# Score tiles in runs of two, three and three, and one shared set of PSUM banks, in a fused attention block

## The chip, the core and the metric

The kernel runs on one core of one Trainium2 chip. The metric is the device time of one execution in microseconds (us). Smaller is better.

## What is computed

Four sequences of 1024 tokens with 1024 features go through conditioned attention with 16 heads, a residual, and a causal convolution with four taps whose taps are the condition vectors:

```python
scale, shift = split(emb @ W_emb + b_emb)
xn = rms_norm(x, g_norm) * (1 + scale) + shift
q, k, v = heads(xn @ W_qkv)                  # 16 heads of 64
q, k = rms_norm(q, g_q), rms_norm(k, g_k)
attn = softmax(q @ k.T * 64 ** -0.5)
o = attn @ v
x = x + (o + o @ W_out)
x = x + causal_conv(x, taps=cond, bias=conv_b)   # 4 taps, per feature
```

Everything is float32.

## The kernel before

**Work.** The projection to q, k and v is done in 16 doubles (four for each sequence, two pairs of heads in each). A double is cut into seven products P1 to P7 of half-size blocks, which are combined by additions, each for four token tiles. That makes 28 pieces, and a piece (`Double.piece`, L638) is one PSUM tile `pqkv` of 128 x 384: eight TensorE instructions, then the additions that empty it (L657 to L669, on ScalarE for P1, on VectorE for the others). Transposes of q and k (`qkt`, L500), transposed inputs (`xtp`, L310), the output projection (`po`, L927 and L1004, begun by the transposed residual of L991) and the transposes ahead of a store (`otp`, L1051) use one PSUM bank each as well. All these tiles come from one pool of three banks, `ps_m`.

**Attention.** It goes in 64 units. A unit p is one pair of heads and one half (512) of the queries of a sequence. The text calls its eight key tiles S0 to S7 where scores are meant, and V0 to V7 where values are.

- `scores` (L683): for each key tile two matmuls, one for each head of the pair, side by side in the halves of the array (64 rows each), into one tile of two PSUM banks (`ps_s`, two such tiles), copied to `sp` in SBUF by ScalarE in one instruction of 128 x 1024 (L696). A running maximum over the key tiles follows on VectorE (L705).
- `softmax` (L732) only plans: the maximum over partitions on GpSimd (L710), its copy into a third use of `ps_s`, called `mbp` (L719), then for each key tile a subtraction on VectorE (L724), an exponential on ScalarE and a running sum on GpSimd (L728, L730).
- `values` (L746): 16 matmuls side by side in the two column halves of the array, into the bank of `ps_a`.
- `finish` (L760): `tot`, the sums over the keys, in a bank of `ps_m`. `spread` (L781) copies them out, `invert` (L791) and `divide` (L799) send the reciprocal through DRAM and multiply.

So PSUM's eight banks are four for `ps_s`, three for `ps_m`, one for `ps_a`.

**Order.** The order of instructions on every compute engine is the order in which the program emits them. The emission is steered by a clock of estimated times: `defer(delay, key, step)` puts a step off, `tick(us)` moves the clock and emits what has come due, `need(key)` emits the named steps at once. A tile of a pool waits until the last reader of the bank's earlier tile is done.

The main loop (L1322 to L1357) emits, for unit p, its scores in four runs of two key tiles, between them the values of unit p-1 (0 to 3, then 4 and 5, then 6 and 7), `finish`, and then, behind the last scores, the fill: the pieces of `between(p)` (L1235), which hold seven projection pieces, transposes, output products and the loads of later ones. `split` (L1273) keeps the last 26 us of the pieces by the clock (22 us for the first 16 units) behind the scores, and what is over is cut into three stretches that go between the runs.

In unit 63 the fill consists of `own`, seven tiles of the output projection of the last sequence. After the loop come the values of unit 63, its `finish` and `divide`, and nine more output tiles. Each output tile is `residual`, two products, two ScalarE instructions that read the bank (`L1019`, `L1033`), and afterwards usually one `otp` of an earlier tile.

Of the kernel before, what the change touches and what calls it, by code (L numbers as in the profile page):

```python
# [15 lines left out]
P = 128  # L16
# [5 lines left out]
def kernel(  # L22
# [53 lines left out]
    small = ctx.enter_context(tc.tile_pool(name="small", bufs=2))  # L76
    ps_s = ctx.enter_context(tc.tile_pool(name="ps_s", bufs=2, space=bass.MemoryType.PSUM))
    ps_m = ctx.enter_context(tc.tile_pool(name="ps_m", bufs=3, space=bass.MemoryType.PSUM))
    dram = ctx.enter_context(tc.tile_pool(name="dram", bufs=1, space=bass.MemoryType.DRAM))
# [62 lines left out]

    turn = [0]

    def evacuate(dst, src):

        turn[0] ^= 1
        if turn[0]:
            nc.scalar.copy(dst, src)
        else:  # L150
            nc.vector.tensor_copy(dst, src)

# [26 lines left out]
    cols_ps = ps_m.tile([P, 512], F32, tag="m", name="cols_ps")  # L179
    nc.tensor.transpose(cols_ps[:, :NR], rows, ident[:NR, :NR])  # L180
# [83 lines left out]
    class Chunk:  # L264
# [31 lines left out]
        def transposes(self, c):  # L296
            b, k, q = self.b, self.k, self.q
            need("xg", self.name)
            if c == 0:
                if len(combining) == 2:  # L300
                    d, *at = combining.pop(0)
                    need(*(("r", d, *at) if d else ("s", *at)))
                combining.append((b, q, k))
                tag, n, bufs = R_HOMES.get((q, k), R_HOME) if b == 0 else R_HOME
                rs = [
                    apool.tile([P, n, QN], F32, tag=tag, name=f"r_{self.name}_{i}", bufs=bufs) for i in range(0, 8, n)
                ]
                self.r = lambda i: rs[i // n][:, i % n, :]
                self.stores = [(rs[i // n][:, : min(n, 7 - i), :], i, min(i + n, 7)) for i in range(0, 7, n)]
            tp = ps_m.tile([P, 2, QN], F32, tag="m", name=f"xtp_{self.name}_{c}")  # L310
# [70 lines left out]
    class Embed:  # L381
# [22 lines left out]
        def run(self):  # L404
            half = self.half
            ps = ps_m.tile([P, 512], F32, tag="m", name=f"mod_ps_{half}")[:, :QN]
            for k in range(NJ):
# [10 lines left out]

            mt = ps_m.tile([P, 512], F32, tag="m", name=f"modT_ps_{half}")[:, :QN]
            mt = mt.rearrange("p (i g b) -> p i g b", i=2, g=4)  # L420
# [27 lines left out]
    class Pair:  # L448
# [51 lines left out]
        def transposes(self, g, s):  # L500

            b, c = self.b, self.c
            need("qk", b, c, g)
            tp = ps_m.tile([P, HN], F32, tag="m", name=f"qkt_{b}_{c}_{g}_{s}")
# [81 lines left out]
    class Double:  # L586
# [39 lines left out]
        def direct(self, c, q):  # L626

            a = self.a[(A11, A12)[c], q] = self.tile_a((A11, A12)[c], q)
            for k in range(KH):
                tp = ps_m.tile([P, 512], F32, tag="m", name=f"xtd_{c}_{q}_{k}")[:, :QN]  # L630
                for i in range(2):
                    nc.tensor.transpose(
                        tp[:, i * P : (i + 1) * P], x0[2 * q + i][c][:, k * P : (k + 1) * P], ident
                    )
                tick(0.22)
                modulate(a[:, k, :], tp, 0, k + c * KH, k % 2 == 1)

        def piece(self, i):  # L638

            name, place, t = self.products[i]  # L640
            px, py = self.pairs
            pm = ps_m.tile([P, 512], F32, tag="m", name=f"pqkv_{self.n}_{name}_{t}")[:, :W3]
            w, a = self.w[name], self.a.get((place, t // 2))
# [33 lines left out]
    class Unit:  # L677
# [5 lines left out]
        def scores(self, kts):  # L683
            pr = self.pr
            for kt in kts:
                ps = ps_s.tile([P, 2, HN], F32, tag="s", name=f"s_{self.name}_{kt}")
                for h in range(2):
                    nc.tensor.matmul(  # L688
                        ps[:, h, :],
                        pr.kT[kt // HT][h * D : (h + 1) * D, kt % HT * P : (kt % HT + 1) * P],  # L690
# [4 lines left out]
                sp = apool.tile([P, 2, HN], F32, tag="sp", name=f"sp_{self.name}_{kt}", bufs=9)  # L695
                nc.scalar.copy(sp, ps)  # L696
                self.sp.append(sp)
# [19 lines left out]
        def broadcast(self):  # L717
            mb = ps_s.tile([P, 2, HN], F32, tag="s", name=f"mbp_{self.name}")
            nc.scalar.copy(mb, self.mb)  # L719
# [177 lines left out]
    class Quad:  # L897
# [29 lines left out]
        def product(self, name):  # L927
# [9 lines left out]
            else:  # L937
                pm = ps_m.tile([P, 512], F32, tag="m", name=f"po_{b}_{j}_{name}")
            for k in range(KH):
# [23 lines left out]
    class Out:  # L963
# [27 lines left out]
        def residual(self, whole=False):  # L991

            self.pm = ps_m.tile([P, 512], F32, tag="m", name=f"po_{self.name}")
            for i in range(HT):
# [56 lines left out]
        def store(self):  # L1051
            b, j, half = self.b, self.j, self.half
            need("y", self.name)
            tp = ps_m.tile([P, 512], F32, tag="m", name=f"otp_{self.name}")
            for i in range(HT):
# [15 lines left out]
    TO_MAX, TO_SPREAD, TO_SHIFT, TO_EXP, STEP = 2.6, 6.5, 7.6, 1.3, 1.8  # L1071
    BEHIND = 26
    SHARES = (0.25, 0.5, 0.25)
    LEADS = ((11, 7), (10, 9))
    LEADS_LAST = ((11, 7), (10, 12))
    DIVIDE = 18.0
    STEP_FIRST = 1.6
    BEHIND_FIRST = 22.0
    LATER = ((0, 0), (4, 0))
# [174 lines left out]

    def cut(pieces, shares):

        ends = list(accumulate(shares))
        total = sum(t for t, _ in pieces)
        stretches, done = [[] for _ in shares], 0.0
        for t, step in pieces:  # L1260
            at = (done + t / 2) / max(total, 1e-9) * ends[-1]
            stretches[next((i for i, e in enumerate(ends) if at < e), len(ends) - 1)].append((t, step))
            done += t
        return stretches
# [8 lines left out]
    def split(pieces, behind):  # L1273

        left, n = behind, len(pieces)
        while n and left > 0:
            n -= 1
            left -= pieces[n][0]
        return cut(pieces[:n], SHARES) + [pieces[n:]]


# [41 lines left out]
    for p in range(B * NB):  # L1323
        unit = Unit(doubles[p // 4].pairs[p // 2 % 2], p % 2)
        stretches = split(between(p), BEHIND if p >= NB else BEHIND_FIRST)
        if p == B * NB - 1:
# [3 lines left out]
            gather(B - 1, 1)  # L1330
            stretches = cut(between(p), SHARES) + [own]
        stretches = iter(stretches)

        def fill():
            run(next(stretches))
# [68 lines left out]
```

## Time and profile before

| | |
|---|---|
| median of 3 runs | 2846.8 us (2844.96 to 2851.01) |
| profiled execution, first to last instruction | 2846.5 us; the page gives no other time of it |
| TensorE (PE) busy | 2764.2 us, 97% |
| VectorE (DVE) busy | 2161.3 us, 76% |
| ScalarE (ACT) busy | 1541.5 us, 54% |
| GpSimd (POOL) busy | 1345.1 us, 47% |
| mean granted TensorE clock | 0.995 |

The profile names an instruction by its engine, its line in the kernel and the tiles it writes and reads. "PE" is a matmul and "PEld" the loading of weights for it. A float32 matmul shows as two TensorE instructions, so a pair of score matmuls for one key tile is four. The chain that ended last goes back from the last instruction to whatever released each step. The list of waits gives, for each group of instructions, the idle time of its engine ahead of it and what ended that. The timeline merges neighbouring instructions of a line and gives their start and the length up to the end of the last one; since matmuls overlap, the time that a run takes is the distance of its start from the start of the next row.

### The profile page before, as it was taken

Reading aid. Unit: us, or ns where it says so; the run is one execution under the profiler, and the core shown is the slowest. Engines: PE = TensorE matmul, PEld = TensorE weight load, DVE = VectorE, ACT = ScalarE, POOL = GpSimd, SP = SyncE. Lnnn points to the kernel's source line nnn. Section 1 sums busy time; section 2 is a strip of 40 time slices with the busy share of each in tenths; the row PEclk is TensorE's granted clock in tenths of the full one; section 3 lists DMA queues with packets and bytes.
Section 4 is the critical chain, followed back from the end, with each engine's and each line's share of the span. In section 5 each row is a group of like instructions: output and inputs, shape, how many; then the busy total and the mean of one; then the engine's idle time right before and its main releaser. Section 6 shows DMA issues by size and latency. Waiting matters only on the chain.

```text
span 2846.5 us, 31973 instructions
## 1 busy us (share of the span) xinstructions
PE 2764.2 (97%) x10581; PEld 1310.7 (46%) x10581; DVE 2161.3 (76%) x2579; ACT 1541.5 (54%) x2221; POOL 1345.1 (47%) x534
## 2 busy tenths in 40 slices
PE   6999999999999999999999999999999999999998
PEld 3544444444444444444444445445444444443344
DVE  4688887888888777777877777787877877687863
ACT  4255656655555556655555556665555545555532
POOL 2056554565654453553555355355445445554520
PEclk9999999999999999999999999999999999999999
DMA  9844555644565566665565556666556444533334
GB/s 318 280 168 145 193 174 184 211 152 169 174 196 159 174 196 205 214 229 164 162 207 186 165 178 212 203 218 198 163 202 211 141 130 159 167 109 96 118 108 118
DMA packets 416844, 509.40 MB, mean 179 GB/s; under 512 B 40816, under 2 KB 326824, under 8 KB 406952
## 3 DMA queue, kind: packets, MB, share of 16 engines
q1 hardware_dynamic: 416680, 507.36, 55.1%
q8 instruction: 85, 1.39, 0.2%
q14 instruction: 79, 0.65, 0.1%
HBM read 411.85 MB, written 95.40 MB: 178 GB/s over the span
## 4 chain that ended last, share of the span: by engine, by line
PE 78%; DVE 11%; DMA 4%; ACT 3%; issue 2%; POOL 2%; SPq 1%; DVEq 0%; ACTq 0%; POOLq 0%
PE pqkv_P L648 29%; PE pav L751 15%; PE s L688 15%; PE po L1009 5%; PE po_P L940 4%; PE po L940 4%; DVE sp L724 3%; DVE mx L705 3%; POOL sum L730 1%; PE qkt L506 1%; PE tot L766 1%; DMA scrR<-few 1%; DVE qk L498 1%; PE po L995 1%; ACT sp L696 1%
## 5 line engine op out<-in xcount | busy, mean ns | idle before, releaser
L648 PE MATMUL pqkv_P<-w_P,a 128*128 128x384 f32 x3456 | 1172.5, 490 | 15.5 <-issue 5.6
L730 POOL TENSOR_TENSOR sum<-sum,sp 128x1024 f32<-128x1024 f32 x384 | 956.8, 2492 | 36.5 <-ACT sp L728 5.7
L648 PEld LDWEIGHTS pqkv_P<-w_P,a 128*128 128x128 f32 x3456 | 639.4, 190 | 478.7 <-issue 69.2
L696 ACT COPY sp<-s 128x1024 f32<-128x1024 f32 x512 | 506.0, 1015 | 507.4 <-PE s L688 459.1
L705 DVE TENSOR_TENSOR mx<-mx,sp 128x1024 f32<-128x1024 f32 x384 | 518.9, 1351 | 170.9 <-ACT sp L696 143.8
L728 ACT ACTIVATE sp<-sp 128x1024 f32<-128x1024 f32 x512 | 531.8, 1055 | 204.6 <-DVE sp L724 201.3
L724 DVE TENSOR_TENSOR sp<-sp,mbp 128x1024 f32<-128x1024 f32 x512 | 604.2, 1210 | 19.3 <-ACT mbp L719 19.3
L710 POOL PARTITION_ALL_REDUCE mb<-mx x64 | 219.2, 3426 | 826.5 <-DVE mx L705 785.0
L688 PE MATMUL s<-qT,kT 64*128 64x512 f32 x2048 | 516.3, 620 | 21.8 <-DVE sp L724 17.0
L751 PE MATMUL pav<-sp,v 128*64 128x512 f32 x2048 | 486.5, 607 | 0.0
L730 POOL TENSOR_TENSOR sum<-sp,sp 128x1024 f32<-128x1024 f32 x64 | 151.5, 2367 | 485.6 <-ACT sp L728 232.9
L688 PEld LDWEIGHTS s<-qT,kT 64*128 64x128 f32 x2048 | 174.9, 186 | 314.8 <-issue 200.0
L751 PEld LDWEIGHTS pav<-sp,v 128*64 128x64 f32 x2048 | 131.2, 137 | 331.9 <-issue 322.2
L1045 DVE SCALAR_TENSOR_TENSOR y<-x,cols,y 128x512 f32<-128x512 f32 x192 | 224.3, 1173 | 47.9 <-ACT y L1033 43.3
L705 DVE TENSOR_TENSOR mx<-sp,sp 128x1024 f32<-128x1024 f32 x64 | 113.2, 1769 | 102.1 <-ACT sp L696 102.0
L667 DVE TENSOR_TENSOR qk<-u,pqkv_P 128x256 f32<-128x256 f32 x256 | 106.2, 415 | 77.9 <-PE pqkv_P L648 76.5
L1009 PE MATMUL po<-ob,wo 128*128 128x512 f32 x352 | 155.3, 593 | 0.0
L940 PE MATMUL po_P<-o_P,wq_P 128*128 128x512 f32 x320 | 143.9, 592 | 0.0
L498 DVE TENSOR_TENSOR qk<-qk,ms 128x1024 f32<-128x1024 f32 x64 | 129.7, 2047 | 0.0
L719 ACT COPY mbp<-mb 128x1024 f32<-128x1024 f32 x64 | 65.2, 1018 | 111.0 <-POOL mb L710 111.0
L940 PE MATMUL po<-o_P,wq_P 128*128 128x512 f32 x240 | 108.0, 592 | 0.0
L485 ACT ACTIVATE sq<-qk 128x512 f32<-128x512 f32 x128 | 76.7, 627 | 53.6 <-DVE qk L667 53.6
(94 smaller groups left out, 1730.7 us busy)
## 6 DMA issues: line engine op xcount, KB each, us to landing
a<-scrA SPq DMA_DIRECT2D x212, 512.0 KB
w_P<-scrB SPq DMA_DIRECT2D x64, 768.0 KB
o_P<-scrS SPq DMA_DIRECT2D x40, 1024.0 KB
w_P<-in_L_cond_W_qkv_dram SPq DMA_DIRECT2D x192, 192.0 KB
o_P<-scrO SPq DMA_DIRECT2D x30, 1024.0 KB
scrA<-r SPq DMA_DIRECT2D x28, 896.0 KB
wq_P<-scrW SPq DMA_DIRECT2D x70, 256.0 KB
xc<-in_x_dram SPq DMA_DIRECT2D x64, 256.0 KB
```

Source lines behind the costliest of these rows:

```text
L648: nc.tensor.matmul(pm, (chunk.r(place) if a is None else a[:, k, :])[:, t % 2 * P : (t % 2 + 1) * P], w[:, k, :], start=(k == 0), stop=(k ...
L688: nc.tensor.matmul(ps[:, h, :], pr.kT[kt // HT][h * D : (h + 1) * D, kt % HT * P : (kt % HT + 1) * P], pr.qT[self.half][h * D : (h + 1) * ...
L696: nc.scalar.copy(sp, ps)
L705: nc.vector.tensor_max(self.mx, self.mx if kt > 1 else self.sp[0], self.sp[kt])
L710: nc.gpsimd.partition_all_reduce(self.mb.rearrange("p h q -> p (h q)"), self.mx.rearrange("p h q -> p (h q)"), P, bass_isa.ReduceOp.max,)
L724: nc.vector.tensor_sub(self.sp[kt], self.sp[kt], self.mb)
L728: nc.scalar.activation(sp, sp, AF.Exp)
L730: nc.gpsimd.tensor_tensor(self.sum, self.sum if kt > 1 else self.sp[0], sp, ALU.add)
L751: nc.tensor.matmul(self.pav[h * D : (h + 1) * D, :], self.pr.v[kt // HT][:, kt % HT, h * D : (h + 1) * D], self.sp[kt][:, h, :], start=(kt ...
L940: nc.tensor.matmul(pm, self.w[name][:, k, :], self.o[name][:, k, :], start=(k == 0 and name not in ("P2", "P3", "P4")), stop=(k == KH - 1),)
L1009: nc.tensor.matmul(self.pm, self.w[kh][:, k % KH, :], oTs[b, k, half], start=False, stop=(k == NJ - 1),)
L1045: nc.vector.scalar_tensor_tensor(self.y, self.x1[:, k : k + HN], cols[:, r : r + 1], self.y, ALU.mult, ALU.add)
```

## The change

- The pools `ps_s` and `ps_m` become one pool in which every bank has a name: `s0` and `s1` (two banks each), `b0`, `b1` and `m` (one each).
- Scores: key tiles 0, 3, 6 use `s1`, key tiles 1, 4, 7 use `s0`, and key tiles 2 and 5 use the two single banks `b0` and `b1`, one for each head, with one copy of 128 x 512 for each instead of one of 128 x 1024.
- `mbp` is always in `s0`.
- All other PSUM tiles come from `bank()`, which goes round a list: all five names up to the first scores, `m` alone during the scores, `m`, `b0`, `b1` in the fill, and `b0`, `b1` from the fill of the last unit to the end.
- The runs are two, three and three key tiles, with values 0 to 3 and 4 to 7 between them, and the whole of `between(p)` comes behind the last scores.
- What is left of the subtractions and exponentials of unit p-1 is emitted ahead of S0, not behind S1. `spread` is emitted with `finish`.

```diff
-    ps_s = ctx.enter_context(tc.tile_pool(name="ps_s", bufs=2, space=bass.MemoryType.PSUM))
-    ps_m = ctx.enter_context(tc.tile_pool(name="ps_m", bufs=3, space=bass.MemoryType.PSUM))
+    psum = ctx.enter_context(tc.tile_pool(name="psum", bufs=1, space=bass.MemoryType.PSUM))
...
+    def double_bank(i, name):
+        return psum.tile([P, 2, 512], F32, tag=f"s{i}", name=name)
+
+    APART = ["m"]
+    FILL = ["m", "b0", "b1"]
+    ALL = FILL + ["s1", "s0"]
+    banks, at_bank = [ALL], [0]
+
+    def use_banks(some):
+        banks[0], at_bank[0] = some, 0
+
+    def bank(name):
+        tag = banks[0][at_bank[0] % len(banks[0])]
+        at_bank[0] += 1
+        if tag[0] == "s":
+            return double_bank(int(tag[1]), name)[:, 0, :]
+        return psum.tile([P, 512], F32, tag=tag, name=name)
...
-            pm = ps_m.tile([P, 512], F32, tag="m", name=f"pqkv_{self.n}_{name}_{t}")[:, :W3]
+            pm = bank(f"pqkv_{self.n}_{name}_{t}")[:, :W3]
...
-                ps = ps_s.tile([P, 2, HN], F32, tag="s", name=f"s_{self.name}_{kt}")
+                name = f"s_{self.name}_{kt}"
+                if kt % 3 == 2:
+                    ps = [psum.tile([P, HN], F32, tag=f"b{h}", name=f"{name}_{h}") for h in range(2)]
+                else:
+                    whole = double_bank(1 - kt % 3, name)
+                    ps = [whole[:, h, :] for h in range(2)]
...
-                nc.scalar.copy(sp, ps)
+                if kt % 3 == 2:
+                    for h in range(2):
+                        nc.scalar.copy(sp[:, h, :], ps[h])
+                else:
+                    nc.scalar.copy(sp, whole)
...
-            mb = ps_s.tile([P, 2, HN], F32, tag="s", name=f"mbp_{self.name}")
+            mb = double_bank(0, f"mbp_{self.name}")
...
-            tot = ps_m.tile([P, HN], F32, tag="m", name=f"tot_{self.name}")
+            tot = bank(f"tot_{self.name}")
...
-            defer(0.2, key, lambda: self.spread(tot))
+            self.spread(tot)
...
-        stretches = split(between(p), BEHIND if p >= NB else BEHIND_FIRST)
+        pieces = between(p)
         if p == B * NB - 1:
...
-            stretches = cut(between(p), SHARES) + [own]
...
+            pieces += own
+
+        use_banks(APART)
+        if last is not None:
+            need("exp", last.name)
         unit.scores((0, 1))
         if last is not None:
-            need("exp", last.name)
             last.values(range(0, HT))
-        fill()
-        unit.scores((2, 3))
-        fill()
+        unit.scores((2, 3, 4))
         if last is not None:
-            last.values(range(4, 6))
-        unit.scores((4, 5))
-        if last is not None:
-            last.values(range(6, NT))
+            last.values(range(HT, NT))
             last.finish()
-        fill()
-        unit.scores((6, 7))
+        unit.scores((5, 6, 7))
+        use_banks(FILL if p < B * NB - 1 else FILL[1:])
         need("mx", unit.name)
         unit.softmax()
...
-        fill()
+        run(pieces)
         last = unit
```

The other tiles of `ps_m` (`xtp`, `qkt`, `po`, `otp` and a few at the start) go over to `bank()` in the same way as `pqkv`.

More of the change, by code (lines that the diff above doesn't have):

```diff
@@ L2 @@
 from contextlib import ExitStack
-from itertools import accumulate, count
+from itertools import count
 import concourse.bass as bass
@@ L141, in need @@
         flush(lambda e: e[2] == key)
[L143 to L151, printed above, removed]
+    def double_bank(i, name):
[12 more added lines that the diff above has]
+        return psum.tile([P, 512], F32, tag=tag, name=name)
     def inverse_root(x, n):
@@ L178 @@
             nc.sync.dma_start(rows[R_GQ + i : R_GQ + i + 1, h * D : (h + 1) * D], g.rearrange("(o d) -> o d", o=1))
-    cols_ps = ps_m.tile([P, 512], F32, tag="m", name="cols_ps")
+    cols_ps = bank("cols_ps")
     nc.tensor.transpose(cols_ps[:, :NR], rows, ident[:NR, :NR])
@@ L309, in transposes @@
                 self.stores = [(rs[i // n][:, : min(n, 7 - i), :], i, min(i + n, 7)) for i in range(0, 7, n)]
-            tp = ps_m.tile([P, 2, QN], F32, tag="m", name=f"xtp_{self.name}_{c}")
+            tp = bank(f"xtp_{self.name}_{c}").rearrange("p (h t) -> p h t", h=2)
             for i in range(4):
@@ L405, in run @@
             half = self.half
-            ps = ps_m.tile([P, 512], F32, tag="m", name=f"mod_ps_{half}")[:, :QN]
+            ps = bank(f"mod_ps_{half}")[:, :QN]
             for k in range(NJ):
@@ L417, in run @@
             nc.scalar.copy(sb, ps)
-            mt = ps_m.tile([P, 512], F32, tag="m", name=f"modT_ps_{half}")[:, :QN]
+            mt = bank(f"modT_ps_{half}")[:, :QN]
             mt = mt.rearrange("p (i g b) -> p i g b", i=2, g=4)
@@ L503, in transposes @@
             need("qk", b, c, g)
-            tp = ps_m.tile([P, HN], F32, tag="m", name=f"qkt_{b}_{c}_{g}_{s}")
+            tp = bank(f"qkt_{b}_{c}_{g}_{s}")
             for i in range(HT):
@@ L629, in direct @@
             for k in range(KH):
-                tp = ps_m.tile([P, 512], F32, tag="m", name=f"xtd_{c}_{q}_{k}")[:, :QN]
+                tp = bank(f"xtd_{c}_{q}_{k}")[:, :QN]
                 for i in range(2):
@@ L685, in scores @@
             for kt in kts:
-                ps = ps_s.tile([P, 2, HN], F32, tag="s", name=f"s_{self.name}_{kt}")
+                name = f"s_{self.name}_{kt}"
[4 more added lines that the diff above has]
+                    ps = [whole[:, h, :] for h in range(2)]
                 for h in range(2):
                     nc.tensor.matmul(
-                        ps[:, h, :],
+                        ps[h],
                         pr.kT[kt // HT][h * D : (h + 1) * D, kt % HT * P : (kt % HT + 1) * P],
@@ L937, in product @@
             else:
-                pm = ps_m.tile([P, 512], F32, tag="m", name=f"po_{b}_{j}_{name}")
+                pm = bank(f"po_{b}_{j}_{name}")
             for k in range(KH):
@@ L991, in residual @@
         def residual(self, whole=False):
-            self.pm = ps_m.tile([P, 512], F32, tag="m", name=f"po_{self.name}")
+            self.pm = bank(f"po_{self.name}")
             for i in range(HT):
@@ L1053, in store @@
             need("y", self.name)
-            tp = ps_m.tile([P, 512], F32, tag="m", name=f"otp_{self.name}")
+            tp = bank(f"otp_{self.name}")
             for i in range(HT):
@@ L1071 @@
     TO_MAX, TO_SPREAD, TO_SHIFT, TO_EXP, STEP = 2.6, 6.5, 7.6, 1.3, 1.8
-    BEHIND = 26
-    SHARES = (0.25, 0.5, 0.25)
     LEADS = ((11, 7), (10, 9))
@@ L1077 @@
     STEP_FIRST = 1.6
-    BEHIND_FIRST = 22.0
     LATER = ((0, 0), (4, 0))
@@ L1253, in between @@
         return [piece for slot in slots for piece in slot]
[L1255 to L1264, printed above, removed]
     def run(pieces):
@@ L1271, in run @@
                 tick(until - clock[0])
[L1273 to L1279, printed above, removed]
     doubles[0] = first = Double(0)
@@ L1330 @@
             gather(B - 1, 1)
-            stretches = cut(between(p), SHARES) + [own]
-        stretches = iter(stretches)
-        def fill():
-            run(next(stretches))
+            pieces += own
+        use_banks(APART)
+        if last is not None:
+            need("exp", last.name)
         unit.scores((0, 1))
         if last is not None:
-            need("exp", last.name)
             last.values(range(0, HT))
-        fill()
-        unit.scores((2, 3))
-        fill()
+        unit.scores((2, 3, 4))
         if last is not None:
-            last.values(range(4, 6))
-        unit.scores((4, 5))
-        if last is not None:
-            last.values(range(6, NT))
+            last.values(range(HT, NT))
             last.finish()
-        fill()
-        unit.scores((6, 7))
+        unit.scores((5, 6, 7))
+        use_banks(FILL if p < B * NB - 1 else FILL[1:])
         need("mx", unit.name)
```

## The prediction

> **What bounds the kernel now.** First the page: engine shares and the chain that ended last.
>
> ```profile
> PE 2764.2 (97%) x10581; PEld 1310.7 (46%) x10581; DVE 2161.3 (76%) x2579; ACT 1541.5 (54%) x2221; POOL 1345.1 (47%) x534
> ...
> PE 78%; DVE 11%; DMA 4%; ACT 3%; issue 2%; POOL 2%; SPq 1%; DVEq 0%; ACTq 0%; POOLq 0%
> ```
>
> TensorE is the bound, yet a fifth of the chain runs through other engines. Where, is told by the waits, of TensorE and then of its weight loads:
>
> ```profile
> PE s L688 <- DVE sp L724: 17.0, 13, 2.2
> ...
> PE tot L766 <- POOL sum L730: 6.9, 4, 3.5
> ...
> PE po L995 <- ACT y L1033: 1.0, 2, 0.5
> ```
>
> ```profile
> PEld s L688 <- DVE sp L724: 31.3, 21, 3.1
> ```
>
> In 21 of the 64 units S1 waits until the last subtraction of the unit before has let go of `mbp`. By the timeline they are units 2 to 8, 12 to 17, 19, 23, 31, 35, 39, 51, 61 and 62. I call them bound by VectorE. The other 42 that follow a unit are bound by TensorE: there the scores, values and `tot` of every unit without an output piece among them take 15.5 us, without a gap. Such a unit, in the timeline of TensorE:
>
> ```profile
> 1521.82 1.99 PE L688 MATMUL s<-qT,kT 64*128 64x512 f32 x8
> 1523.74 3.65 PE L751 MATMUL pav<-sp,v 128*64 128x512 f32 x16
> 1527.32 1.99 PE L688 MATMUL s<-qT,kT 64*128 64x512 f32 x8
> 1529.24 1.94 PE L751 MATMUL pav<-sp,v 128*64 128x512 f32 x8
> 1531.11 1.99 PE L688 MATMUL s<-qT,kT 64*128 64x512 f32 x8
> ```
>
> Read starts: 16 instructions of values take 3.58 us, 8 take 1.87, so a second run costs 0.16 us more than going on. Eight of scores take 1.92. A unit bound by VectorE shows four by themselves:
>
> ```profile
> 618.90 1.13 PE L688 MATMUL s<-qT,kT 64*128 64x512 f32 x4 [1.34 <-DVE sp L724]
> 619.96 3.65 PE L751 MATMUL pav<-sp,v 128*64 128x512 f32 x16
> ...
> 631.11 0.64 PE L766 MATMUL tot<-sum,ones 128*32 128x256 f32 x8
> 631.68 1.99 PE L688 MATMUL s<-qT,kT 64*128 64x512 f32 x8
> ```
>
> That is 1.06 us, so four more in a run cost 0.86.
>
> **Fewer runs.** Behind the first run a unit now has three runs of eight for scores (3 x 1.92 = 5.76) and 3.58 + 1.87 + 1.87 = 7.32 for values. Then it has two of twelve (2 x 2.78 = 5.56) and two of sixteen (7.16). The difference is 0.36 us. It counts where TensorE is the bound: 42 x 0.36 = **-15.1 us**. The pieces that stand between the runs in units 24, 25, 40 and 41 add one or two changes of form each; at 0.18 us for a change (half of 0.36), **-1.0**.
>
> **Units bound by VectorE.** Here the loop goes from S1 through the last maximum, GpSimd's reduction and the eight subtractions to the next S1, and VectorE has work without a gap from the last maxima on. So the place of the last maximum behind S1 decides. In the unit above, from the timeline of VectorE:
>
> ```profile
> 633.96 2.56 DVE L705 TENSOR_TENSOR mx<-mx,sp 128x1024 f32<-128x1024 f32 x2 [0.84 <-ACT sp L696]
> ```
>
> It ends at 636.52, 17.6 us behind S1. After the change: S1 1.06, V0-3 3.58, S2-4 2.78, V4-7 3.58, so `tot` starts at 11.00 (before: 12.21) and S5, 0.57 later, at 11.57. The copy of a tile starts 1.23 after its first matmul (S6: 631.68 to 632.91), hence 12.80. Two copies of 128 x 512 from PSUM, 0.58 each and 0.48 apart when in sequence, with some 0.07 over one of 1.01 in all, end at 13.88. Three maxima 1.33 apart end at 17.8, because they now come in a burst. That is 0.19 later, not 0.36 earlier: 16 units that wait clearly (without 5, 31, 35, 51 and 62, whose waits are under 0.4) x 0.19 = **+3.0**. An upside I leave to the range: `invert` falls due 0.9 us of the clock earlier, and VectorE's waits for the reciprocal's DMA (37 us in all) could shrink.
>
> The Trainium skill, "Perfetto Trace Analysis", section Optimizing Scalar/DVE Operations, says that ScalarE pays about 51 ns for each access to PSUM and that larger operations pay better, which speaks against the split copy. The row (two in sequence against one) gives 0.07; by the rule the same sum changes by under half a microsecond, and ScalarE is 54% busy.
>
> **`tot` comes 1.21 us earlier.** It needs GpSimd's last sum. Behind it are S5 to S7 on TensorE and the copies on ScalarE, where `spread` now stands ahead of copy 5. The timeline's distance from the last sum to `tot` is 0.4, 0.05, 1.0, 0.05, 0.05, 0.8 and 1.0 us in units 1, 2, 3, 5, 6, 14 and 17, and at least 1.7 in all others but the last unit, whose `tot` stays where the sum puts it. What is missing to 1.21 is a new wait: 0.8 + 1.2 + 0.2 + 1.2 + 1.2 + 0.4 + 0.2 = **+5.2**.
>
> **Subtractions ahead of S0.** In most units they have been emitted by then, so it costs nothing. In unit 18 S1 now uses the bank pair of S0's copy (806.96) and not that of the last subtraction (ended 809.00). With names, S1 always needs `mbp`'s pair: **+2.2** with the 0.19 of above. In unit 63 the same is covered by the wait for the sum.
>
> **Banks of the fill.** S2 now needs `b0` and `b1`, so the additions that empty the fill's last tiles. In every unit they end at least 1.3 us before S2, mostly over 4, so nothing; without that cover it would be VectorE's delay one for one. The fill's first tile waits for `spread` (done 2 us before it), its second and third for copies 5 (13.9 behind S1, the fill begins at 14.4): nothing. Inside the fill there are three banks as before; a bank's next user comes 1.7 us or more after it was emptied in the steady units that I followed (1536 to 1650 us). The first pieces of a fill issue their loads behind the scores now; `spread`'s transfers, on which SyncE's queue waits 763 us in all, are released some 3 us earlier, and a load has four or more pieces (10 us) until its use. Up to the first scores there are five banks in place of three: the waits there (about 5 us, bounds 0 and -5) end in a wait for `w_P` from DRAM of 1.8 us, which lands when it lands; I take **-0.4**, for the one behind it.
>
> **The tail.** From the fill of the last unit on two banks are left. The tail's rows:
>
> ```profile
> 2743.07 1.02 PE L1009 MATMUL po<-oT,wo 128*128 128x512 f32 x2
> ...
> 2743.93 0.60 PE L1056 MATMUL otp<-ident,y 128*128 128x128 f32 x4
> 2744.13 0.59 ACT L1019 COPY x<-po 128x512 f32<-128x512 f32 x1 [3.79 <-PE po L1009]
> 2744.36 0.60 PE L995 MATMUL po<-ident,xc 128*128 128x128 f32 x4
> 2744.61 0.78 ACT L1033 ACTIVATE y<-po,cols,tap_self 128x512 f32<-128x512 f32 x1
> ```
>
> With one `otp` for each output tile, `po` is always in one bank and `otp` in the other, so the next residual (2744.36) waits for L1033's end (2745.39) and 0.05 for the semaphore: 1.08 us. Where two `po` follow each other it costs nothing. Through the 16 tiles in order: 1.5 at the second (two `otp` and ScalarE's copy of `mbp` ahead), 1.2 at the fourth, where L1033 ends at 2731.45, 3 x 1.08 up to the values, 0.6 behind a double `otp`, 6 x 1.08 at the end: **+13.0**. Nothing lies beside it: TensorE has almost no gap here.
>
> Skill, same page, section Optimization Strategy: equal bubbles that repeat on the engine that should be full can mean too few buffers in PSUM. Before, two of 0.48 us are all there is of it here.
>
> **Sum.** -15.1 - 1.0 + 3.0 + 5.2 + 2.2 - 0.4 + 13.0 = +6.9 us. The profiled span (2846.5) stands 0.3 under the median, so I add it to the median: 2853.7. A difference of 0.2%, 5.7 us, is about what a measurement of this kernel can tell from none.
>
> **Rivals.**
> - *Faster: the bound units save as well.* If VectorE's burst of maxima has slack behind it (less filler work, the earlier reciprocal), the 21 units gain 0.36 too (-7.6), and the +3.0 and the +5.2 fall away: 2838. It decides once the last maximum comes earlier behind S1, not later. For it: VectorE idles 2 to 3 us ahead of maxima in such units. Against: none of that idle time lies behind copy 5.
> - *About even: the tail isn't paid.* If the rotation meets two `po` in a row more often than I read, it is up to 13.0 less: 2841. Against: the order in the rows is plain.
> - *Much slower: tile 5's banks hold up the fill.* If copies 5 end late behind exponentials, the second tile of each fill waits; at one change's worth, 0.35 us in 63 units, +22: 2876; in half of them 2865. It decides once the copies end over 3 us later than worked out. Against: copies 5 to 7 end at most 1.8 us after their matmul's start now.
> - *The change doesn't do what it says*: excluded, the emission is by hand.
>
> **How the numbers follow.** The forecast has a chance of 0.50 (0.33 slower, 0.15 within, 0.02 faster), the gain everywhere 0.20 (0.15 faster, 0.05 within), the unpaid tail 0.13 (0.05 and 0.08), the held banks 0.17, all slower. Faster 0.22, same 0.28, slower 0.50. The range goes from the gain everywhere, 2838, to 2866, where half of the fills wait.
>
> **What would show it.** Right: scores in rows of x12 lasting 2.8 us from start to start; steady units shorter by 0.36; a new line of waits, `po` L995 for ACT's y L1033, near 11 us; `tot`'s wait for GpSimd near 12; the wait of S1 for VectorE no smaller. Wrong: a wait of fill tiles for copies of scores, a shorter span between 160 and 845 us, or a tail (from the last unit's `tot`) that keeps its 146 us.

## The result, and the profile after

The changed kernel takes 2866.1 us (median of 5 runs, 2865.0 to 2869.6) where the kernel before takes 2846.8 (5 runs, 2844.2 to 2851.0): ratio 1.0066, interval 1.0054 to 1.0078. Run once more, it gave 1.0062 [1.0039, 1.0086]. It is slower, as the forecast had it, but by 19 us (16 to 19, as the two comparisons give it) where the sum had said 6.9; the time lies at the upper end of the range, 2866, an end that the prediction had from a rival (held banks) which did not come about. The profiled execution has a span of 2864.3 us (before: 2846.5).

From the page of the changed kernel, the busy times and the shares of the chain that ended last:

```profile
PE 2751.2 (96%) x10581; PEld 1327.3 (46%) x10581; DVE 2167.2 (76%) x2579; ACT 1551.4 (54%) x2349; POOL 1344.6 (47%) x534
...
PE 76%; DVE 12%; DMA 4%; POOL 2%; issue 2%; ACT 2%; SPq 1%; DVEq 0%; POOLq 0%; ACTq 0%
```

TensorE is busy for 13 us less than before, yet the span is 18 us longer. ScalarE has its 128 split copies more and 10 us more work. So TensorE's work did get shorter, and something else took the place. TensorE's waits (us in total, how many, the longest):

```profile
PE s L703 <- DVE sp L743: 23.6, 12, 5.2
PE po L1014 <- ACT y L1052: 10.8, 10, 2.5
...
PE tot L785 <- POOL sum L749: 4.6, 4, 2.7
...
PE po L1028 <- DVE oT L825: 2.0, 1, 2.0
```

The first line is S1 waiting for the bank pair of `mbp` (17.0 before). The second is the one that the prediction announced: the tail's residuals wait for ScalarE's second reading of the bank (1.0 before). `tot`'s wait did not grow (6.9 before), and the last line is new.

A unit that TensorE bounds, in its timeline after the change:

```profile
1531.68 1.99 PE L703 MATMUL s<-qT,kT 64*128 64x512 f32 x8
1533.60 3.65 PE L770 MATMUL pav<-sp,v 128*64 128x512 f32 x16
1537.18 2.85 PE L703 MATMUL s<-qT,kT 64*128 64x512 f32 x12
1539.96 3.65 PE L770 MATMUL pav<-sp,v 128*64 128x512 f32 x16
1543.54 0.64 PE L785 MATMUL tot<-sum,ones 128*32 128x256 f32 x8
1544.11 2.85 PE L703 MATMUL s<-qT,kT 64*128 64x512 f32 x12
1546.89 2.85 PE L658 MATMUL pqkv_P<-w_P,a 128*128 128x384 f32 x8
```

From S0 to the fill it goes 15.21 us by starts (the distance from S0's start to S7's end fell from 15.63 to 15.28); three scores take 2.78.

Where the time went is told by stages, cut at the first score matmul of a unit. In brackets stands the number of **half-clock windows**: the records of the granted clock show TensorE at 0.50 for exactly 3.41 us, or a multiple of it, now and then. All numbers in us, each from one profile:

| | start to S0 of unit 0 | units 0 to 19 | units 20 to 60 | unit 61 to the end | span |
|---|---|---|---|---|---|
| before | 127.1 (1) | 759.6 (4) | 1714.3 (0) | 245.5 (4) | 2846.5 |
| after | 129.5 (4) | 767.3 (8) | 1707.1 (1) | 260.4 (4) | 2864.3 |
| after, again | 131.5 (3) | 775.3 (11) | 1704.4 (0) | 262.0 (5) | 2873.1 |

One window of each last stage is that in which the execution ends. The units in the middle gained 7 to 10 us, the tail lost 15 to 17, and the first third lost 8 to 16, in step with its windows. (Four profiles have the same program in units 0 to 19: these two, and the first two of the experiments below, with 774.9 us and 10 windows, and 764.9 us and 5.)

### The profile page after: what moved, and what is told of

The parts are those of the page before. It is cut to its first block, busy times and chain, and to the rows that moved or that the text cites. A ratio compares the mean times of both kernels' runs of the same rounds, so it can differ in the third digit from the quotient of the medians.

```text
span 2864.3 us, 32140 instructions
## 1 busy us (share of the span) xinstructions
PE 2751.2 (96%) x10581; PEld 1327.3 (46%) x10581; DVE 2167.2 (76%) x2579; ACT 1551.4 (54%) x2349; POOL 1344.6 (47%) x534
## 4 chain that ended last, share of the span: by engine, by line
PE 76%; DVE 12%; DMA 4%; POOL 2%; issue 2%; ACT 2%; SPq 1%; DVEq 0%; POOLq 0%; ACTq 0%
PE pqkv_P L658 29%; PE pav L770 15%; PE s L703 14%; PE po L1028 5%; PE po_P L959 4%; PE po L959 3%; DVE sp L743 3%; DVE mx L724 3%; POOL sum L749 2%; DVE qk L508 2%; PE qkt L516 1%; PE tot L785 1%; DMA rec<-scrR 1%; PE po L1014 1%; DMA we<-in_L_cond_W_emb_dram 1%
## 5 line engine op out<-in xcount | busy, mean ns | idle before, releaser
L724 DVE TENSOR_TENSOR mx<-mx,sp 128x1024 f32<-128x1024 f32 x384 | 512.3, 1334 | 178.3 <-ACT sp L713 148.3
L703 PE MATMUL s<-qT,kT 64*128 64x512 f32 x2048 | 499.0, 614 | 24.4 <-DVE sp L743 23.6
L770 PE MATMUL pav<-sp,v 128*64 128x512 f32 x2048 | 472.3, 604 | 0.0
L715 ACT COPY sp<-s 128x1024 f32<-128x1024 f32 x384 | 377.9, 1028 | 140.6 <-PE s L703 92.3
L703 PEld LDWEIGHTS s<-qT,kT 64*128 64x128 f32 x2048 | 181.9, 187 | 295.0 <-issue 228.4
L1064 DVE SCALAR_TENSOR_TENSOR y<-x,cols,y 128x512 f32<-128x512 f32 x192 | 234.3, 1225 | 53.3 <-ACT y L1052 48.8
L713 ACT COPY sp<-s 128x512 f32<-128x512 f32 x256 | 137.5, 589 | 172.5 <-PE s L703 172.5
L508 DVE TENSOR_TENSOR qk<-qk,ms 128x1024 f32<-128x1024 f32 x64 | 136.1, 2145 | 0.0
L738 ACT COPY mbp<-mb 128x1024 f32<-128x1024 f32 x64 | 65.1, 1017 | 123.4 <-POOL mb L729 123.4
L803 ACT COPY tots<-tot 128x256 f32<-128x256 f32 x62 | 23.1, 373 | 175.3 <-PE tot L785 175.3
```

The lines of the kernel that those rows point to most:

```text
L703: nc.tensor.matmul(ps[h], pr.kT[kt // HT][h * D : (h + 1) * D, kt % HT * P : (kt % HT + 1) * P], pr.qT[self.half][h * D : (h + 1) * D, :], ...
L715: nc.scalar.copy(sp, whole)
L724: nc.vector.tensor_max(self.mx, self.mx if kt > 1 else self.sp[0], self.sp[kt])
L770: nc.tensor.matmul(self.pav[h * D : (h + 1) * D, :], self.pr.v[kt // HT][:, kt % HT, h * D : (h + 1) * D], self.sp[kt][:, h, :], start=(kt ...
L1064: nc.vector.scalar_tensor_tensor(self.y, self.x1[:, k : k + HN], cols[:, r : r + 1], self.y, ALU.mult, ALU.add)
```

## The experiments

After the result two things were held against each other: that the loss sits in the tail's two banks, in S1's wait for `mbp` and in the start (theory A in what follows, with its prices), and that the runs of three themselves, or something common to all stages, hurt. Three edits of the changed kernel each take one suspected cost away, and one puts the runs of scores back. They share their runs of the kernel before (median 2851.5 of 19).

### A third bank in the tail

```diff
-        use_banks(FILL if p < B * NB - 1 else FILL[1:])
+        use_banks(FILL if p < B * NB - 1 else FILL[1:] + ["s1"])
```

> The changed kernel with a third bank, s1, for the fill of the last unit and the tail. From the fill of the last unit to the end the changed kernel takes 18.8 us more than the one before (from -1.0 to +17.8). Theory A (a wait costs itself and, where TensorE was idle for some 2 us, a window of 3.41 us at half clock on top, 1.7 us): all waits of the residuals for L1052 go, and so does the window at 2735; what stays is the wait of 2.0 us for oT. So about 16 us less: 2850. Theory B (only the waits that the prediction listed count, and the surplus comes from somewhere else): 13.0 less, 2853. Rival: the tail is bound by ScalarE and VectorE: under 8 less.

Measured: 2855.2 us, ratio 1.0017 [1.0002, 1.0032]. The stage from unit 61 to the end takes 244.1 us, 16.3 less than with two banks. Its list of waits has again

```profile
PE po L1028 <- DVE oT L825: 2.0, 1, 2.0
...
PE po L1014 <- ACT y L1052: 1.0, 2, 0.5
```

Of the ten waits of 10.8 us only the two of 1.0 that the kernel before has are left, and the slow restarts are gone; the wait for `oT` stays. The two banks cost 16 us, as theory A had it for this stage. The whole kernel gained only 11 against the 2866.1 of above: in this profile units 0 to 19 took 7.6 us more than in the first one of the changed kernel, with 10 half-clock windows in place of 8.

### Three banks at the start

```diff
-    banks, at_bank = [ALL], [0]
+    banks, at_bank = [FILL], [0]
```

> The changed kernel with three banks (m, b0, b1) up to the first scores in place of five. Theory A: with five banks TensorE arrives earlier at the wait for w_P from DRAM, is idle longer there and gets four windows at half clock in place of one; with three, S0 of unit 0 comes 2.4 us earlier (127.1, not 129.5) and one window is left. Theory B: the banks make no difference, since w_P lands when it lands: S0 of unit 0 within 0.5 us of 129.5.

Measured: one run of 2865.6 us; the first scores begin at 129.0, so in this run the start gained 0.5 us, with one half-clock window in place of four. Theory A was right on the windows and wrong on the time, which is theory B's. The reason for the windows stands in the timelines of TensorE, first with five banks:

```profile
64.85 1.94 PE L322 MATMUL xtp<-ident,x 128*128 128x128 f32 x8 [4.16 <-DVE v L677]
...
70.43 5.46 PE L658 MATMUL pqkv_P<-w_P,r 128*128 128x384 f32 x8 [3.64 <-DMA w_P<-scrB]
```

and with three:

```profile
66.18 2.39 PE L322 MATMUL xtp<-ident,x 128*128 128x128 f32 x16 [3.07 <-DVE v L677]
71.37 2.99 PE L658 MATMUL pqkv_P<-w_P,r 128*128 128x384 f32 x5 [2.79 <-DMA w_P<-scrB]
```

With five banks TensorE gets sooner to the wait for weights from DRAM and waits longer there; the weights come when they come, and the eight products behind it then take 5.46 us at half the clock. Over all runs, kernels with five banks start their first scores at 128.2 to 131.5 (six profiles), those with three at 126.9 to 129.0 (five), and the two kernels with forced idle further below, which have three banks as well, at 131.1 and 132.3. So the loss of 2 us at the start is not shown to come from the banks.

### Runs of two again

```diff
-        unit.scores((2, 3, 4))
+        unit.scores((2, 3))
         if last is not None:
-            last.values(range(HT, NT))
+            last.values(range(HT, 6))
+        unit.scores((4, 5))
+        if last is not None:
+            last.values(range(6, NT))
             last.finish()
-        unit.scores((5, 6, 7))
+        unit.scores((6, 7))
```

> The changed kernel's banks with the order of the kernel before: runs of two key tiles, values 0 to 3, 4 and 5, 6 and 7 between them. Theory A: the steady units (20 to 60) lose their 0.35 us each, some +14 in that stage; units 0 to 19 keep their time within 3 us, because the subtractions decide there and half-clock windows come by chance of the idle's length. Rival: the runs of three (tot earlier, maxima in a burst) made units 0 to 19 slower: that stage gets 6 to 8 us shorter. In all 2866 + 14 against 2866 + 7.

Measured: 2877.9 us, ratio 1.0100 [1.0084, 1.0116]. Units 20 to 60 take 1716.1 us, 9 more than with runs of three, where 14 were expected; units 0 to 19 take 770.0 with 9 half-clock windows, against 767.3 with 8. So the runs of three are worth 9 us in the middle and take nothing in the first third. The rival, that they are what hurts the units bound by VectorE, falls.

### S0 alone ahead of the values

```diff
-        unit.scores((0, 1))
+        unit.scores((0,))
...
-        unit.scores((2, 3, 4))
+        unit.scores((1, 2, 3, 4))
```

> Runs of one, four and three: S0, values 0 to 3, S1 to S4, values 4 to 7, tot, S5 to S7, on the changed kernel's banks. S1 then comes 3.6 us later and no longer waits for the last subtraction. Theory A: the 23.6 us that TensorE waits there go, with some five half-clock windows of 1.7 us behind them, and GpSimd's sum becomes the limit of the same units: tot waits more. Together 12 to 20 us less, about 2850. Rival (VectorE is the bound of these units, so S1's wait only moves, to tot or to the fill's banks): units 0 to 19 within 3 us of the changed kernel.

S0 uses `s1`; `mbp` is in `s0`, which S1 needs. Now V0 to V3 stand between. Measured: 2856.4 us, ratio 1.0021 [1.0010, 1.0033], 10 us less than the changed kernel where theory A had 12 to 20; units 0 to 19 take 760.3 us, 7.0 less with as many windows (8), units 20 to 60 2.1 less with one fewer. The list of waits:

```profile
PE tot L785 <- POOL sum L749: 9.1, 3, 6.8
...
PE pav L770 <- DVE oT L825: 3.7, 6, 1.8
...
PE s L703 <- ACT sp L715: 3.4, 1, 3.4
```

The 23.6 us of S1 for the subtraction are gone; what came in their place is smaller.

### The three edits together, and `tot` later

> Three edits on the changed kernel at once: runs of one, four and three key tiles (e4), a third bank from the fill of the last unit on (e1), three banks up to the first scores (e2). If the three are independent: 2866 less 16 (the tail, measured in e1 by stage) less 9 (units 0 to 60 of e4) = 2841, 0.2 to 0.4% under the kernel before. If they share a cause (half-clock windows that only move to another place): 2847 or more.

Measured: 2840.3 us (7 runs), ratio 0.9957 [0.9942, 0.9972] to the kernel before (here 2850.3, 16 runs): faster than both kernels. The edits add up.

To that version, next, `finish` behind S5 to S7 in every unit, with the fill beginning on `b0` so that `tot` has `m` for itself:

```diff
-            last.finish()
         unit.scores((5, 6, 7))
+        if last is not None:
+            last.finish()
```

> e5 with tot behind S5 to S7, and the fill's tiles in the order b0, b1, m. The last maxima come 0.6 us earlier behind S1 and GpSimd's last sum has 2.7 us more until tot. Theory A: waits of tot for the sum (9.1 us in e4, 6.8 of it in the last unit) go in units 0 to 20, and that stage gets 3 to 8 us shorter than in e5; units 20 to 60 as in e5. Rival: VectorE is the bound of units 0 to 20, so tot's place changes nothing: within 2 us of e5.

Measured: 2855.3 us, ratio 1.0022 [1.0010, 1.0033]. Both expectations missed. Most steps from one unit to the next behind unit 20 are the same to 0.2 us, but those of units 6, 16, 26 and 42 are 4.4 to 7.8 us longer. The timeline of VectorE in unit 26, and then of TensorE:

```profile
1190.83 0.69 DVE L825 TENSOR_TENSOR oT<-pav,rec 128x512 f32<-128x512 f32 x1 [4.27 <-DMA rec<-scrR]
1191.43 0.41 DVE L677 TENSOR_TENSOR qk<-u,pqkv_P 128x256 f32<-128x256 f32 x1
1191.76 0.28 DVE L677 TENSOR_TENSOR v<-u,pqkv_P 128x128 f32<-128x128 f32 x1
```

```profile
1192.14 1.09 PE L322 MATMUL xtp<-ident,xg 128*128 128x128 f32 x4 [3.81 <-issue]
```

`tot` and with it the reciprocal come later, but `divide` is emitted at the same time of the clock as before. It waits 4.27 us for the reciprocal's DMA and holds up the additions behind it, and these hold a fill bank that TensorE wants 0.1 us after they are done (the profile names no releaser for that row; that the addition is it, I read from the times). VectorE's waits for this DMA go from 28.0 us in all to 65.1.

The division also holds the bank of `pav`, which the next unit's values need. In unit 16 it waits 7.25 us for the DMA and TensorE waits 7.51 us for it ahead of V0. Over the kernel this is the largest of TensorE's waits, 5.4 us in all without the move and with it

```profile
PE pav L770 <- DVE oT L825: 19.2, 7, 7.5
```

What made unit 6 longer was not followed.

So only the last unit is worth trying, where nothing of the loop follows and `tot` waits 8.6 us:

```diff
-            last.finish()
+            if p < B * NB - 1:
+                last.finish()
         unit.scores((5, 6, 7))
+        if p == B * NB - 1:
+            last.finish()
```

> The version with all three edits (three banks at the start, S0 alone first, three banks in the tail), and in the last unit alone tot behind S5 to S7. There tot waits 8.6 us for GpSimd's last sum, and S5 to S7 (2.8 us) stand behind it. Theory A: the wait shrinks to 5.8 and the kernel by 2 to 3 us, to about 2837. Rival B (the tail is then bound by what hangs on the last unit's maxima, or a tile of the output projection waits for tot's reciprocal): within 1 us of 2840.

Measured: 2835.2 us (5 runs, 2833.6 to 2836.1), ratio 0.9943 [0.9924, 0.9962] to the kernel before (here 2853.4, 9 runs). The wait is down to 6.0, and the stage from unit 61 to the end takes 242.0 us where the version before it took 244.5, with as many windows (4):

```profile
PE tot L785 <- POOL sum L749: 8.7, 4, 6.0
```

That is 34 us less than the changed kernel beside it (2869.7). Theory A fits, but by whole times this version can't be told from the one before it: their intervals to the kernel before overlap.

### What idle time costs

The windows had no place in the sum. Two kernels put an idle stretch of TensorE into the steady units 26 to 45 of the kernel before, ahead of S0: a transpose, copies in sequence on ScalarE that need it, and a transpose that needs these (3 copies or 13).

```diff
+    idle_sb = const.tile([P, 8], F32, name="idle_sb")
+    nc.vector.memset(idle_sb, 0.0)
...
+        if 26 <= p < 46:
+            pp = ps_m.tile([P, 512], F32, tag="m", name=f"probe_{p}")
+            nc.tensor.transpose(pp[:, :P], ident, ident)
+            nc.scalar.copy(idle_sb, pp[:, :8])
+            for _ in range(3):
+                nc.scalar.copy(idle_sb, idle_sb)
+            pq = ps_m.tile([P, 512], F32, tag="m", name=f"probe2_{p}")
+            nc.tensor.transpose(pq[:8, :P], idle_sb, ident)
+            nc.scalar.copy(idle_sb[:8, :], pq[:8, :8])
```

> The kernel before with a forced idle of TensorE ahead of S0 in units 26 to 45 (a transpose, five tiny ScalarE copies in a row, a transpose that reads the last): about 1.2 to 1.5 us idle in each of 20 units that had no wait. Both theories: 24 to 32 us more in all (the idle and two transposes); theory A: at most two windows at half clock in that stretch.

> The same with fifteen tiny copies, about 3 us idle in each of the 20 units. Theory A (an idle of 2.5 us or more mostly brings a window of 3.41 us at half clock behind it): 60 us for the idles and 12 to 18 windows of 1.7 us, 20 to 30 us more: 80 to 90 in all. Theory B (a wait costs itself): 60 to 65 in all.

Measured: with the short idle (0.94 us) the plain units grow by 1.33 us and none of these gaps is followed by a window; units 30, 34, 38 and 43 grow by 3.7 to 5.9 and units 31, 35 and 39, ahead of which the gap is 3.2 to 4.8, by 2.9, from collisions that I did not follow. So the stage grows by 45.7 us with 5 windows, more than the expectation had (24 to 32 and at most two), and the total says nothing. With the long one (3.23 us) the units 27, 28, 37, 43 and 44 have no window and grow by 3.6 to 3.9, the units 32, 33, 36 and 40 to 42 have one and grow by 5.3: a half-clock window costs **1.65 us** (5.26 less 3.61) where TensorE is busy (half of 3.41 is 1.71). The stage has 19 of them and grows by 109 us, more than either theory had. The scores behind a forced gap (of 5.16 us in this unit), with a window, in the timeline of TensorE (eight take 1.99 otherwise):

```profile
1394.71 0.37 PE L1346 MATMUL probe<-ident,idle_sb 128*8 128x128 f32 x1 [5.16 <-ACT idle_sb L1344]
1395.01 3.79 PE L690 MATMUL s<-qT,kT 64*128 64x512 f32 x8
```

The other way round: products that nobody reads are put into the changed kernel between S0 and S1 in eleven units where S1 waits (`WARM` says how many for each, 1 to 5), so that TensorE idles less and nothing comes earlier. The changed kernel ran beside it.

```diff
-        unit.scores((0, 1))
+        unit.scores((0,))
+        if p in WARM:
+            warm = bank(f"warm_{p}")
+            for _ in range(WARM[p]):
+                nc.tensor.matmul(
+                    warm, unit.pr.kT[0][:, :P], unit.pr.qT[unit.half], start=True, stop=True
+                )
+        unit.scores((1,))
```

> The changed kernel once more, to stand beside the next run under the same conditions. Both theories: about 2866 us, a granted clock of 0.990 to 0.991, that is some 16 half-clock windows of 3.41 us, of which five follow a wait of S1 for the subtraction (at 698, 776, 817 and two at 2684 us in the first profile).

> The changed kernel with products that nobody reads between S0 and S1, in the eleven units in which S1 waits (1 to 5 products of 128 x 512, each no longer than 0.9 us, fewer than fill the wait). S1 can start no earlier than without them, so by everything but the clock the time stays or grows by a few tenths. Theory A (the idle time of TensorE brings the windows, and the windows are what the forecast lacked): the windows behind S1's waits go, about five of 1.65 us each, so 6 to 9 us less than the changed kernel and a granted clock higher by 0.002 to 0.003. Rival B (windows come whatever the idle time, or cost nothing in units that wait for VectorE): the time within 2 us of the changed kernel's, the clock the same.

Measured: 2864.7 us with the idle products, 2869.7 without, 4.9 less by medians and 3.9 by mean spans, with a clock of 0.991 to 0.993 against 0.989 to 0.990. The clocks of the two don't overlap, so that the windows go with the idle time is shown; the gain in time is not clear of the noise (a 95% interval of about -1 to 9 us for the 3.9). Unit 17 in the timeline of TensorE, without (the first profile of the changed kernel):

```profile
775.84 1.88 PE L703 MATMUL s<-qT,kT 64*128 64x512 f32 x4 [1.78 <-DVE sp L743]
777.65 1.98 PE L770 MATMUL pav<-sp,v 128*64 128x512 f32 x4
```

and with:

```profile
772.20 1.13 PE L1337 MATMUL warm<-qT,kT 128*128 128x512 f32 x2
774.00 1.13 PE L704 MATMUL s<-qT,kT 64*128 64x512 f32 x4 [0.67 <-DVE sp L744]
775.06 3.65 PE L771 MATMUL pav<-sp,v 128*64 128x512 f32 x16
```

Four scores take 1.81 us from start to start after an idle of 1.78 us, and 1.06 after one of 0.67. The busy times by stretches (PE, PEld, DVE, ACT, POOL, then the granted clock) say the same, without and with:

```profile
776.00:781.00 5.00, 5.00 (x16) 1.29 (x18) 0.23 (x1) 2.79 (x3) 4.84 (x3) 0.66 0.47 170
```

```profile
774.00:779.00 5.00, 5.00 (x22) 1.66 (x24) 1.71 (x1) 2.95 (x3) 4.84 (x3) 1.00 0.46 170
```

The step from unit 17 to 18 takes 39.8 us without, 40.4 in the second profile without, and 38.1 with. The gain was to be 6 to 9; it fell short in part in unit 23, whose product waited 2.65 us for the bank of a fill tile and made the step about 4 us longer.

## Why the prediction was right, and where its size was off

The direction was right, and the largest loss of the sum, the tail's two banks, cost what the sum had and 3 us more. That units 0 to 19 come near as well is luck, and so is a time inside the range, whose upper end had another reason. The terms add up to -0.4 us at the start, +8.1 in units 0 to 19, -13.6 in units 20 to 60 and +12.8 behind them; the first two profiles differ by +2.4, +7.7, -7.2 and +14.9. Two things had no term in the sum.

**The clock was left out.** The sum was made at the clock of the profile of before, 0.995, and the step "Sum" adds its terms as if it stayed. Every run reports its mean granted clock c, so (1 - c) x span is the clock that it lost: 17.7 us on average over 44 runs of the kernel before, 29.5 over 10 runs of the changed one. Within each kernel of the study, runs that lose 1 us more of it are 0.84 us longer (standard error 0.06). The mean spans are 2849.1 and 2866.8, 17.7 apart; 0.84 x 11.8 = 9.9 us of that go with the clock, and 7.8 are left, where the sum says 6.9. This is a split by correlation: a longer wait lengthens a run by itself as well as by its window. The forced idle shows the price of a window alone, and with the idle products that windows come from idle time.

**The waits of the fill were left out.** The prediction has "Inside the fill there are three banks as before", read from 1536 to 1650 us alone, and puts nothing. In units 0 to 60 of the first two profiles, TensorE's gaps over 0.1 us ahead of scores and `tot` are 19.9 us before and 20.8 after. Those ahead of the fill's tiles go from 22.3 to 38.2. From the lists of waits, before and then after:

```profile
PE pqkv_P L648 <- issue: 5.6, 3, 2.6
PE xtp L312 <- DVE v L667: 4.9, 4, 3.1
```

```profile
PE pqkv_P L658 <- issue: 10.1, 5, 4.2
...
PE xtp L322 <- DVE v L677: 7.8, 6, 4.2
PE qkt L516 <- DVE u L670: 5.1, 4, 1.9
```

The last line has no counterpart before. With runs of two on the same banks the sum of the fill is 28.2, so 10 of the 16 us came with the runs of three; why the fill then waits more was not tested. In units 0 to 19 these waits and four more windows took the place of +9.9 for the burst, `tot` and unit 18, whose waits there grew by 0.1 in all. The terms one by one:

- **Fewer runs (-15.1) and pieces (-1.0).** The size for a unit was right: units without anything else went down by 0.35, e.g. from 42.44 to 42.09 us a step. But units 20 to 60 gave 7 to 10 us in all where 14 of the sum lay (36 of the 42 units, and the pieces); the waits of the fill grew by 4.7 there. In units 25 and 41 a transposed input now waits 1.26 us for VectorE, and their steps grew by 1.26 us or more; four steps (28, 32, 44, 48) gained only 0.17.
- **Burst of maxima (+3.0).** Right in kind: the last maximum ends 3.36 us behind the end of S7 where it ended 2.84 behind a S7 that was 0.35 later, 0.17 us in the balance. The waits ahead of scores in units 0 to 60 grew by 0.6 in all (16.5 to 17.1).
- **`tot` earlier (+5.2).** It did not come: 4.6 us of waits against 6.9 before. GpSimd's last sum of unit 1 ended 32.8 us behind S7 in place of 34.7, of unit 2 32.5 in place of 33.9. The first exponentials ended at the same distance as before, within 0.1 in unit 1 and 0.4 in unit 2, while the first sum started 0.9 and 1.4 us sooner. Why GpSimd starts sooner is not settled.
- **Unit 18 (+2.2).** The wait came, 2.47 us, with a half-clock window behind it: the step grew by 2.8, and unit 17's by 2.7.
- **Banks of the fill (0).** No wait of fill tiles for copies of scores is in the list; that rival fell. The waits that did grow are those of above.
- **Start (-0.4).** In the first profiles it cost 2.4 us, with three windows more; that the five banks are the reason is not shown.
- **The tail (+13.0).** Its two banks cost 16. The timeline of the changed kernel, VectorE at the first output tile, and TensorE there and at the fourth and fifth:

```profile
2704.34 3.87 DVE L724 TENSOR_TENSOR mx<-mx,sp 128x1024 f32<-128x1024 f32 x3
2708.13 3.35 DVE L823 RECIPROCAL rec<-tot 128x512 f32<-128x512 f32 x1
```

```profile
2712.26 1.12 PE L1028 MATMUL po<-oT,wo 128*128 128x512 f32 x2 [2.00 <-DVE oT L825]
...
2734.06 0.66 PE L1014 MATMUL po<-ident,xc 128*128 128x128 f32 x4 [2.54 <-ACT y L1052]
2734.55 7.87 PE L1028 MATMUL po<-ob,wo 128*128 128x512 f32 x14
...
2744.63 0.66 PE L1014 MATMUL po<-ident,xc 128*128 128x128 f32 x4 [0.92 <-ACT y L1052]
2745.12 6.17 PE L1028 MATMUL po<-ob,wo 128*128 128x512 f32 x14
```

The reciprocal that the last rows of `oT` need stands behind the burst of maxima, and TensorE waits 2.00 us for it; the sum had the burst in the units but not here. At the fourth tile the wait is 2.54 where the sum had 1.2 (2.7 from residual to residual, since the products start up slowly behind a gap), and the window behind it makes fourteen products 7.87 us long in place of 6.17. At most of the others the gap is 0.92, 1.14 from residual to residual, where the sum had 1.08: that term was read rightly from the rows of before.

- **The rivals.** "The bound units save as well" is half true: steps bound by S1's wait did not, taken together, get shorter, but the run of three is not what hurts them, as the runs of two showed. "The tail isn't paid" fell at its stage.

The Trainium skill, "TensorE: Matmul & The Clock Gate", section "What's actually happening", says that the array falls to half its clock behind an idle window of about 3.4 us. The records agree with the half and with 3.41 us as a grid; they differ on the idle time, since gaps well under 3.4 us were followed by windows too (the last section has the counts). The measurement decides.

## What to carry to other kernels

A sum made of row durations holds only at the granted clock of the rows; for every wait that a change adds or lengthens on TensorE, add a share of 1.65 us for the window that may follow (an estimate; the next section has the chances by length). A reading that a bank never waits holds for the units in which it was read, and the units with other work need their own. A bank count for the tail is worked out from who reads a bank last, as here, and a single bank more was worth 16 us. Before an operation is moved ahead or back, look at what is emitted by a clock of estimates behind it: `divide` didn't move with `tot`, and that cost more than `tot`'s waits ever had.

## What the runs showed of the hardware

How often an idle stretch of TensorE is followed by a half-clock window, by its length, counted over eleven profiles (both kernels and all experiments but the two with forced idle; a window counts when it starts within the gap or up to 1.5 us behind it, and gaps of the first 20 us are left out):

| idle, us | 0.7 to 1.0 | 1.0 to 1.5 | 1.5 to 2.0 | 2.0 to 2.5 | 2.5 to 3.4 | over 3.4 |
|---|---|---|---|---|---|---|
| followed by a window | 0 of 173 | 9 of 119 | 10 of 65 | 18 of 42 | 28 of 37 | 42 of 48 |

The length alone gives chances because the place of the gap decides the rest. All windows of a profile start on one grid of 3.413 us, to 3 ns. Cut into the slots of that grid, the thirteen profiles (from 20 us on) have 10365 slots at full clock in which TensorE idles for less than 1.4 us in all: none is followed by a half-clock slot. Of 138 with 1.4 to 2.1 us, 33 are; of 115 with 2.1 us or more, all. In the long forced idle the same 3.23 us fell as 1.40 and 1.84 us into two slots ahead of unit 27, which has no window, and as 0.80 and 2.43 ahead of unit 32, which has one.

Which stretch is hit changes from run to run, and that goes with much of the spread of one kernel: of 44 runs of the kernel before, those at a clock of 0.996 and 0.997 have spans of 2839 to 2846 us, those at 0.992 of 2850 to 2858. One change of form between score and value runs costs 0.18 us (a score run and a value run fewer: 0.35). Splitting a copy of 128 x 1024 from PSUM on ScalarE in two of 128 x 512 (589 ns each, 0.48 apart, against 1028) costs some 0.04 us in sequence.
